# The experts' down product of a 256-slot block as seven products of halves instead of eight

## The chip, the core and the metric

The kernel runs on one core of a Trainium2 chip. The metric is the device time of one execution in microseconds. A core has five engines with queues of their own, each working in program order: TensorE (PE in the profile, its weight loads PEld), VectorE (DVE), ScalarE (ACT), GpSimd (POOL) and SyncE (SP). POOL and SP mostly issue DMAs here, which run on 16 shared DMA engines.

## The reference, cut to what matters

A two-layer network on 4 images of 32 x 32 tokens with 384 channels. The change lies in the feed-forward part of layer 0, a mixture of four experts of which each token takes two:

```python
def _L0_ffn_ref(x, gate_w, gate_b, w1, b1, w2, b2):
    ...
    topk_vals, topk_idx = jax.lax.top_k(probs, TOP_K)
    ...
    h = jax.nn.gelu(jnp.einsum('bsd,edh->ebsh', x, w1) + b1[:, None, None, :], approximate=False)
    y = jnp.einsum('ebsh,ehd->ebsd', h, w2) + b2[:, None, None, :]
    out = jnp.einsum('bse,ebsd->bsd', masked, y)
    return out
```

The hidden width is 1536. All numbers are float32. "Up" below is the product with `w1`, "down" the product with `w2`.

## The kernel before

The kernel runs attention of layer 0, then the experts, then layer 1 (`outlook`, and a last feed-forward part). The experts compute only the two chosen experts of each token. Every (token, expert) pair has a slot; slots of one expert lie together, in blocks of `XB` = 256, and there are `NXB` = 35 blocks. All 35 are run, one after another, by the loop over `n` in `experts` (from L1587 on).

What a block takes:

- `weights(n)` (L1524): two gathers by POOL bring the expert's `up` weights (128 x 4620 float32) and its `down` weights with the bias (128 x 4992 float32, 2.56 MB). There are two sets of these buffers, used in turn (`halves[n % 2]`), so weights of block n+2 can be fetched when their buffer is no longer read by block n.
- `tokens`, `fetch` (L1535, L1545): POOL gathers the slots' token numbers and the 256 rows of `x1` into `xb`.
- `norm` (L1554) on DVE scales them; `turn` (L1564, L1565) turns them on PE by six 128 x 128 transposes and copies them with DVE into `xbT`.
- Up: for each of the `NF` = 12 slices of 128 hidden units three products of 256 columns (L1607) into `ps_h`, then ACT's Gelu (L1611) into `h`. A float32 product is two matmul instructions, so this is 72 instructions.
- Down: for each half `t` of the block (128 slots) twelve products of 384 columns into one `ps_y` (L1624), 24 instructions a half. The stationary side is a 128 x 128 piece of `h`, the moving side a slice of `down`. DVE adds the bias (L1629), SP sends the half to `yg` in DRAM (L1630). `norm(n + 1)` stands ahead of the down part in DVE's queue, `turn(n + 1)` between the two halves in PE's.

Beside this run other pieces of work. In blocks 0 to 2, `beside` steps finish the attention's output and the routing (DVE L756 to L760 and others; the products L284 on PE). From block 16 on, once all blocks that a tile of 128 tokens needs are written, each block ends up with one `add(i)` (L1571 to L1578): SP loads a tile `x` of `x1` (L1572), POOL gathers the two experts' rows `yt` from `yg` (L1490), DVE forms the weighted sum (L1576, twice) and its statistics (L133, L134), and SP stores it (L1578) at the start of the next block. There are 19 such tiles in blocks 16 to 34; the rest is added in layer 1.

PE, DVE, ACT and SP keep the order in which the program is written (`manual_schedule`); POOL's order is chosen when the program is built. An instruction waits for its operands on its own engine's queue, and everything behind it on that engine waits too. So the order inside the loop matters: `add` is written before the up part, and its DVE instructions stand ahead of everything that DVE does later in the block.

Of the kernel before, what the change touches and what calls it, by code (L numbers as in the profile page):

```python
# [10 lines left out]
FP = mybir.dt.float32  # L11
BF = mybir.dt.bfloat16
AF = mybir.ActivationFunctionType
ALU = mybir.AluOpType
# [3 lines left out]
P = 128  # L18
B, IMG, C = 4, 32, 384
# [3 lines left out]
KC = C // P  # L23
# [3 lines left out]
NE, HID = 4, 1536  # L27
NF = HID // P
# [15 lines left out]
XB = 256  # L44
NXB = (2 * NT * P + NE * (XB - 1)) // XB
NFIRST = 4


class Net:
# [55 lines left out]
    def store(self, x):  # L105
        for b in range(B):
            self.nc.sync.dma_start(
                out=x[b * NTOK : (b + 1) * NTOK, :].rearrange("(t p) c -> p t c", p=P), in_=self.xs[b]
            )
# [1386 lines left out]
def experts(net, router, x1, x2, wup, wdown, beside):  # L1496

    tc, nc = net.tc, net.nc
    TT = XB // P
    I32 = mybir.dt.int32
    with ExitStack() as ctx:
        def pool(name, bufs, **kw):
            return ctx.enter_context(tc.tile_pool(name=name, bufs=bufs, reuse_waits="tile", **kw))


        halves = [pool(f"ex_{n}", 1) for n in range(2)]
        hp, work = pool("ex_h", 14), pool("ex_work", 4)
        ps_h, ps_y = pool("ex_ps_h", 3, space=PSUM), pool("ex_ps_y", 3, space=PSUM)

        def rows(n):
            w, t = router.firsts if n < NFIRST else router.all
            return w[:, n : n + 1], t[:, n : n + 1]

        def weights(n):  # L1520
            up = halves[n % 2].tile([P, KC * HID + NF], FP, name="up", tag="up")
            down = halves[n % 2].tile([P, NF * C + C], FP, name="down", tag="down")
            for t, w in ((up, wup), (down, wdown)):
                nc.gpsimd.indirect_dma_start(  # L1524
                    out=t, out_offset=None, in_=w,
                    in_offset=bass.IndirectOffsetOnAxis(ap=rows(n)[0], axis=0),
                )
            return up, down

        beside = beside(work)  # L1530
        ids, xbs = {}, {}

        def tokens(n):
            t = ids[n] = halves[0].tile([P, TT, router.LINE], I32, name="ids", tag="ids", bufs=6)
            nc.gpsimd.indirect_dma_start(  # L1535
                out=t.rearrange("p t w -> p (t w)"), out_offset=None,
                in_=net.table.rearrange("(r t) w -> r (t w)", t=TT),
                in_offset=bass.IndirectOffsetOnAxis(ap=rows(n)[1], axis=0),
            )

        def fetch(n):
            xb = xbs[n] = halves[n % 2].tile([P, TT, C], FP, name="xb", tag="xb")
            last = (B - 1 if n < NFIRST else B) * NTOK
            for t in range(TT):
                nc.gpsimd.indirect_dma_start(  # L1545
                    out=xb[:, t, :], out_offset=None, in_=x1[:last, :],
                    in_offset=bass.IndirectOffsetOnAxis(ap=ids[n][:, t, 0:1], axis=0),
                )

        def norm(n):  # L1550
            xb = xbs[n]
            own = ids.pop(n).bitcast(FP)
            for t in range(TT):
                nc.vector.tensor_scalar(  # L1554
                    xb[:, t, :], xb[:, t, :], own[:, t, 1:2], own[:, t, 2:3], ALU.subtract, ALU.mult
                )

        def turn(n):
            xb = xbs.pop(n)
            xbT = halves[n % 2].tile([P, KC, XB], FP, name="xbT", tag="xbT")  # L1560
            for t in range(TT):
                ps = router.psum()
                for c in range(KC):
                    nc.tensor.transpose(ps[:, c * P : (c + 1) * P], xb[:, t, c * P : (c + 1) * P], net.ident)  # L1564
                nc.vector.tensor_copy(  # L1565
                    xbT[:, :, t * P : (t + 1) * P], ps[:, :C].rearrange("p (c t) -> p c t", c=KC)
                )
            return xbT

        def add(i):  # L1570
            x = work.tile([P, C], FP, name="x", tag="x", bufs=2)  # L1571
            nc.sync.dma_start(out=x, in_=x1[i * P : (i + 1) * P, :])  # L1572
            for n in range(2):
                y = work.tile([P, C], FP, name="yt", tag="yt")
                router.gather(y, i, n)
                nc.vector.scalar_tensor_tensor(x, y, router.weight[n][:, i : i + 1], x, ALU.mult, ALU.add)  # L1576
            net.measure(work, i, x)
            return lambda: nc.sync.dma_start(out=x2[i * P : (i + 1) * P, :], in_=x)  # L1578

        added, store = 0, lambda: None  # L1580
        ws = {0: weights(0)}
        for n in range(NFIRST):
            tokens(n)
        fetch(0)
        norm(0)
        xbT = turn(0)
        for n in range(NXB):  # L1587
            if n == NFIRST - 1:
                for _ in beside:
                    pass  # L1590
            if n + 1 < NXB:
                if n + 1 >= NFIRST:
                    tokens(n + 1)
                ws[n + 1] = weights(n + 1)
                fetch(n + 1)
            store()
            store = lambda: None
            if n > router.complete(added // NB):
                store = add(added)
                added += 1  # L1600
            up, down = ws.pop(n)
            hs = []
            for f in range(NF):
                ps = ps_h.tile([P, XB], FP, name="ps_h", tag="h")
                for k in range(KC):
                    o = k * HID + f * P
                    nc.tensor.matmul(  # L1607
                        ps, lhsT=up[:, o : o + P], rhs=xbT[:, k, :], start=k == 0, stop=k == KC - 1,
                    )
                h = hp.tile([P, XB], FP, name="h", tag="h")  # L1610
                nc.scalar.activation(h, ps, AF.Gelu, bias=up[:, KC * HID + f : KC * HID + f + 1])  # L1611
                hs.append(h)
                if n < NFIRST - 1 and (n or f >= NF // 2):
                    next(beside, None)
            if n + 1 < NXB:
                norm(n + 1)
            else:
                net.scale(0, added)
            for t in range(TT):
                if t == TT - 1 and n + 1 < NXB:  # L1620
                    xbT = turn(n + 1)
                ps = ps_y.tile([P, C], FP, name="ps_y", tag="y")
                for f in range(NF):
                    nc.tensor.matmul(  # L1624
                        ps, lhsT=hs[f][:, t * P : (t + 1) * P], rhs=down[:, f * C : (f + 1) * C],
                        start=f == 0, stop=f == NF - 1,
                    )
                y = work.tile([P, C], FP, name="y", tag="y")
                nc.vector.tensor_tensor(y, ps, down[:, NF * C :], ALU.add)  # L1629
                nc.sync.dma_start(  # L1630
                    out=net.yg[n * XB : (n + 1) * XB, :].rearrange("(p t) c -> p t c", t=TT)[:, t, :], in_=y
                )
        store()
        return added

# [463 lines left out]
def metaformer_kernel(  # L2099
# [139 lines left out]
```

## Time and profile before

| what | number |
|---|---|
| median of 3 runs | 2905.45 us (2903.23 to 2907.56) |
| profiled execution, device time | 2905.3 us |
| its span, first to last instruction | 2903.6 us, 37519 instructions |
| mean granted PE clock | 0.965 |
| busy: PE, PEld | 2715.6 us (94%), 1453.0 us (50%) |
| busy: DVE, ACT, POOL | 1347.6 us (46%), 1208.3 us (42%), 401.3 us (14%) |
| DMA moved | 405.97 MB, mean 140 GB/s |
| experts, first up product to end of last down product | 1210.6 to 2345.6 us |

The page's busy time of an engine is the union of its instructions' times. The mean duration of a matmul in it contains the time in which it passes through the array while the next has begun, so the step from one matmul to the next is read from busy time over count, or from the starts in the timeline. A row of the groups reads: line, engine, operation, output <- inputs, shapes, count, busy time, mean duration, idle time of the engine just before, and what ended most of it. Idle time of an engine costs nothing unless another waits for it.

### The profile page before, as it was taken

What the parts mean: (1) busy time and instruction counts of PE and PEld (TensorE: products, weight loads), DVE (VectorE), ACT (ScalarE), POOL (GpSimd) and SP (SyncE); (2) the same over time, 40 slices, a digit from 0 to 9 for tenths busy, and PEclk for the clock granted to TensorE, in tenths of its full rate; (3) what the DMA queues carried; (4) which work ended last, traced back from release to release, by engine and by line L of the source; (5) the groups of instructions that cost most, each with busy time, mean ns of one, the idle gap of its engine ahead of it and who ended that gap; (6) DMA issues with size and microseconds to landing.
All of it is one profiled execution on the core that took longest, in us unless ns stands there. A gap on an engine that the chain in (4) does not pass through costs nothing. (4 is left out here: it accounts for less than half of the span.)

```text
span 2903.6 us, 37519 instructions
## 1 busy us (share of the span) xinstructions
PE 2715.6 (94%) x13632; PEld 1453.0 (50%) x13632; DVE 1347.6 (46%) x3714; ACT 1208.3 (42%) x2023; POOL 401.3 (14%) x500
## 2 busy tenths in 40 slices
PE   6889998999999987799999999999999999999988
PEld 3323333333333322367777777777777754444432
DVE  1377776777778786532010001111111146877642
ACT  3778777787778774212112111211211122122135
POOL 1000000120021004122111122212121101100000
PEclk9989999999999998799999999999999999999998
DMA  5143435222413334445545455555555437644432
GB/s 104 32 103 100 100 92 140 66 59 70 109 44 75 80 90 128 130 149 201 190 169 195 168 200 204 200 212 201 214 202 204 162 132 222 193 161 155 145 106 89
DMA packets 216996, 405.97 MB, mean 140 GB/s; under 512 B 83505, under 2 KB 177905, under 8 KB 203745
## 3 DMA queue, kind: packets, MB, share of 16 engines
q1 hardware_dynamic: 185504, 189.20, 22.2%
q0 software_dynamic: 27152, 209.66, 21.1%
q10 hardware_dynamic: 4144, 4.61, 0.5%
q8 instruction: 110, 1.80, 0.3%
q14 instruction: 86, 0.70, 0.1%
HBM read 305.35 MB, written 49.99 MB: 122 GB/s over the span
## 5 line engine op out<-in xcount | busy, mean ns | idle before, releaser
L1611 ACT ACTIVATE h<-ps_h,up 128x256 f32<-128x256 f32 x420 | 199.0, 474 | 916.5 <-PE ps_h L1607 916.4
L1607 PE MATMUL ps_h<-xbT,up 128*128 128x256 f32 x2520 | 553.5, 380 | 2.6 <-ACT h L1611 1.8
L1624 PE MATMUL ps_y<-down,h 128*128 128x384 f32 x1680 | 554.5, 487 | 0.0
L1607 PEld LDWEIGHTS ps_h<-xbT,up 128*128 128x128 f32 x2520 | 479.9, 191 | 77.9 <-ACT h L1611 2.7
L685 DVE CUSTOM_DVE_ANT_0 e<-e,rz,inv 128x1024 f32<-128x1024 f32 x384 | 475.2, 1274 | 51.8 <-DMA rz<-r_row 49.2
L633 ACT ACTIVATE e<-ps_s,ten 128x1024 f32<-128x1024 f32 x384 | 408.1, 1109 | 59.8 <-PE ps_s L623 36.2
L1624 PEld LDWEIGHTS ps_y<-down,h 128*128 128x128 f32 x1680 | 317.3, 191 | 207.0 <-issue 1.2
L1629 DVE TENSOR_TENSOR y<-ps_y,down 128x384 f32<-128x384 f32 x70 | 39.0, 557 | 718.1 <-PE ps_y L1624 718.1
L623 PE MATMUL ps_s<-q,k 32*128 32x512 f32 x1536 | 295.5, 667 | 53.4 <-ACT e L633 31.5
L641 PE MATMUL ps_o<-e,wv 128*32 128x512 f32 x1536 | 226.1, 664 | 40.5 <-DVE wv L692 39.0
L641 PE MATMUL ps_z<-e,rt_ones 128*32 128x512 f32 x1536 | 218.6, 643 | 0.0
L712 POOL DMA_DIRECT2D q<-po x96 | 76.1, 878 | 946.4 <-DMA q<-po 514.6
L369 ACT ACTIVATE below<-tk_left,tk_bound 128x1024 bf16<-128x1024 f32 (+1 forms) x160 | 184.3, 1152 | 52.3 <-DVE tk_bound L375 42.1
L623 PEld LDWEIGHTS ps_s<-q,k 32*128 32x128 f32 x1536 | 92.0, 189 | 192.2 <-ACT e L633 92.0
L1735 PE MATMUL ps_a<-wa,xnT 128*128 128x486 f32 x384 | 167.6, 585 | 8.7 <-DVE attn L1745 7.0
L284 PE MATMUL ps_t<-xnT,wqkv 128*128 128x512 f32 x288 | 137.1, 617 | 2.4 <-ACT xnT L466 1.7
L641 PEld LDWEIGHTS ps_o<-e,wv 128*32 128x32 f32 x1536 | 31.5, 111 | 199.7 <-issue 68.4
L1735 PEld LDWEIGHTS ps_a<-wa,xnT 128*128 128x128 f32 x384 | 71.7, 192 | 93.4 <-issue 85.3
L641 PEld LDWEIGHTS ps_z<-e,rt_ones 128*32 128x32 f32 x1536 | 52.3, 117 | 132.0 <-issue 128.7
L1576 DVE SCALAR_TENSOR_TENSOR x<-yt,weight,x 128x384 f32<-128x384 f32 x38 | 23.5, 619 | 188.3 <-DMA x<-x 187.6
L1837 PE MATMUL ps_y<-band,v 128*32 128x194 f32 (+2 forms) x960 | 102.7, 517 | 8.0 <-DMA band<-room 7.7
L1490 POOL DMA_INDIRECT yt<-yg,index x64 | 65.5, 1024 | 305.9 <-DVE x L1576 142.4
(346 smaller groups left out, 2739.5 us busy)
## 6 DMA issues: line engine op xcount, KB each, us to landing
band<-room SPq DMA_DIRECT2D x32, 1560.0 KB
rz<-r_row SPq DMA_DIRECT2D x48, 512.0 KB
yg<-y SPq DMA_DIRECT2D x70, 192.0 KB
q<-q SPq DMA_DIRECT2D x192, 64.0 KB
k<-k SPq DMA_DIRECT2D x192, 64.0 KB
room<-none SPq DMA_DIRECT2D x64, 192.0 KB
x<-x SPq DMA_DIRECT2D x38, 192.0 KB
o<-in_x_dram SPq DMA_DIRECT2D x33, 192.0 KB
```

Source lines behind the costliest of these rows:

```text
L284: nc.tensor.matmul(ps, lhsT=lhsT(k), rhs=rhs(k), start=k == 0, stop=k == KC - 1)
L369: nc.scalar.activation(junk[:n], left[:n], AF.Sign, bias=bound[:n], accum_out=over[:n])
L623: nc.tensor.matmul(ps[:, half * 512 : half * 512 + 512], lhsT=self.k4[r, u * P : (u + 1) * P], rhs=self.q4[r, :], start=True, stop=True,)
L633: nc.scalar.activation(e, ps, AF.Exp, bias=shift, scale=QK_SCALE)
L641: nc.tensor.matmul(ps[r : r + 32, :], lhsT=lhsT(odd), rhs=self.es[2 * u + odd][:, half * 512 : half * 512 + 512], start=u == 0, stop=u == ...
L685: nc.vector.tensor_tensor_reduce(self.es[m], self.es[m], self.rz, 1.0, self.im["inv"][:, m, self.h : self.h + 1], ALU.mult, ALU.add, self. ...
L712: nc.gpsimd.dma_start(out=there, in_=po[r : r + 32, :], accum_op=ALU.add)
L1607: nc.tensor.matmul(ps, lhsT=up[:, o : o + P], rhs=xbT[:, k, :], start=k == 0, stop=k == KC - 1,)
L1611: nc.scalar.activation(h, ps, AF.Gelu, bias=up[:, KC * HID + f : KC * HID + f + 1])
L1624: nc.tensor.matmul(ps, lhsT=hs[f][:, t * P : (t + 1) * P], rhs=down[:, f * C : (f + 1) * C], start=f == 0, stop=f == NF - 1,)
L1735: nc.tensor.matmul(pa[:, hh, :HW_], lhsT=xnT[:, k, :], rhs=wa[:, k, hh * HW_ : (hh + 1) * HW_], start=k == 0, stop=k == KC - 1,)
L1837: nc.tensor.matmul(ys[c][32 * n : 32 * n + 32, lo - 512 * half : hi - 512 * half], lhsT=vs[b, t][:, h * HD : (h + 1) * HD], rhs=bands[b, t ...
```

## The change

With the block's `h` cut into halves of slots (t) and of hidden units (c), and `down` into halves of hidden units (k) and of output columns (c), the down part is a product of two 2 x 2 matrices of blocks: eight products of 128 slots x 768 hidden units x 192 columns. Before, they are done as 24 float32 products of 384 columns. After, seven products of 192 columns (12 matmul instructions each) are done, on sums of quarters:

- `folded(down)`: four sums of weight quarters (`t1` to `t4`, 128 x 1152 each) and the difference of the two bias halves (`shift`), on DVE, at the start of the block's up part, behind `add`.
- `paired(one, two, g)`: four sums of quarters of `h` (128 x 384 each), twice a block, on DVE: for hidden slices 0-2 with 6-8, and for 3-5 with 9-11. The up part takes the slices in the order 0-2, 6-8, 3-5, 9-11, so that the first pair is there after six of twelve slices.
- `total`: nine sums of 128 x 192 on DVE put the products together, seven of them reading a product's PSUM tile (three such tiles, as before).
- `h` is kept as tiles of three slices, five of them; `y` in two tiles by name.
- The first half of `y` is sent after the fifth product, which is followed by `turn(n + 1)`; the second after the seventh.
- The `down` buffer is read by the first, second and fifth product, by `folded` and by the first `total`; products three, four, six and seven read the sums.

```diff
-        hp, work = pool("ex_h", 14), pool("ex_work", 4)
+        hp, work, sums = pool("ex_h", NG3 + 1), pool("ex_work", 4), pool("ex_sums", 1)
...
+        def folded(down):
+            w11, w12, w21, w22 = (quadrant(down, k, c) for k in range(2) for c in range(2))
+            t = sums.tile([P, 4, HF, D], FP, name="wsum", tag="wsum")
+            t1, t2, t3, t4 = (t[:, i] for i in range(4))
+            nc.vector.tensor_tensor(t1, w12, w11, ALU.subtract)
+            nc.vector.tensor_tensor(t2, w22, t1, ALU.subtract)
+            nc.vector.tensor_tensor(t3, w22, w12, ALU.subtract)
+            nc.vector.tensor_tensor(t4, w21, t2, ALU.subtract)
...
+        def paired(one, two, g):
+            s = sums.tile([P, 4, 3, P], FP, name=f"hsum_{g}", tag=f"hsum_{g}")
+            a11, a21, a12, a22 = (h[:, :, t * P : (t + 1) * P] for h in (one, two) for t in range(TT))
+            s1, s2, s3, s4 = (s[:, i] for i in range(4))
+            nc.vector.tensor_tensor(s1, a21, a22, ALU.add)
+            nc.vector.tensor_tensor(s2, s1, a11, ALU.subtract)
+            nc.vector.tensor_tensor(s4, a12, s2, ALU.subtract)
+            nc.vector.tensor_tensor(s3, a11, a21, ALU.subtract)
+            return s
...
             up, down = ws.pop(n)
-            hs = []
-            for f in range(NF):
+            w11, w21, w22, t1, t2, t3, t4, shift = folded(down)
+            hs, ss = [None] * NG3, []
+            for f in (*range(0, 3), *range(6, 9), *range(3, 6), *range(9, 12)):
...
+                if f in (8, 11):
+                    g = len(ss)
+                    ss.append(paired(hs[g], hs[g + 2], g))
...
-            for t in range(TT):
-                if t == TT - 1 and n + 1 < NXB:
-                    xbT = turn(n + 1)
-                ps = ps_y.tile([P, C], FP, name="ps_y", tag="y")
-                for f in range(NF):
-                    nc.tensor.matmul(
-                        ps, lhsT=hs[f][:, t * P : (t + 1) * P], rhs=down[:, f * C : (f + 1) * C],
-                        start=f == 0, stop=f == NF - 1,
-                    )
-                y = work.tile([P, C], FP, name="y", tag="y")
-                nc.vector.tensor_tensor(y, ps, down[:, NF * C :], ALU.add)
...
+            def product(left, right):
+                ps = ps_y.tile([P, D], FP, name="ps_y", tag="y")
+                for f in range(HF):
+                    nc.tensor.matmul(ps, lhsT=left[f], rhs=right[:, f, :], start=f == 0, stop=f == HF - 1)
+                return ps
...
+            total(c21, product(a(0, 0), w11), down[:, NF * C : NF * C + D])
+            total(c11, product(a(1, 0), w21), c21)
+            total(c22, product(s(0), t1), shift)
+            total(c21, product(s(1), t2), c21)
+            total(c12, c21, c22)
+            total(c12, product(s(3), w22), c12)
+            send(0)
+            if n + 1 < NXB:
+                xbT = turn(n + 1)
+            total(c21, product(s(2), t3), c21)
+            total(c22, c21, c22)
+            total(c21, product(a(1, 1), t4), c21)
+            send(1)
```

More of the change, by code (lines that the diff above doesn't have):

```diff
@@ L1506, in experts @@
     I32 = mybir.dt.int32
+    D, HF = C // 2, NF // 2
+    NG3 = NF // 3
     with ExitStack() as ctx:
@@ L1578, in add, with quadrant @@
             return lambda: nc.sync.dma_start(out=x2[i * P : (i + 1) * P, :], in_=x)
+        def quadrant(down, k, c):
+            w = down[:, : NF * C].rearrange("p (k f c d) -> p k f c d", k=2, f=HF, c=2)
+            return w[:, k, :, c, :]
+        def folded(down):
[6 more added lines that the diff above has]
+            nc.vector.tensor_tensor(t4, w21, t2, ALU.subtract)
+            shift = sums.tile([P, D], FP, name="shift", tag="shift")
+            low, high = (down[:, NF * C + c * D : NF * C + (c + 1) * D] for c in range(2))
+            nc.vector.tensor_tensor(shift, high, low, ALU.subtract)
+            return w11, w21, w22, t1, t2, t3, t4, shift
+        def paired(one, two, g):
[7 more added lines that the diff above has]
+            return s
         added, store = 0, lambda: None
@@ L1609, in experts @@
                     )
[L1610 to L1613, printed above, removed]
+                if f % 3 == 0:
+                    hs[f // 3] = hp.tile([P, 3, XB], FP, name="h", tag="h")
+                nc.scalar.activation(
+                    hs[f // 3][:, f % 3, :], ps, AF.Gelu, bias=up[:, KC * HID + f : KC * HID + f + 1]
+                )
+                if n < NFIRST - 1 and (n or f % 6 >= 3):
                     next(beside, None)
+                if f in (8, 11):
+                    g = len(ss)
+                    ss.append(paired(hs[g], hs[g + 2], g))
             if n + 1 < NXB:
@@ L1618, in experts, with a, s, total @@
                 net.scale(0, added)
-            for t in range(TT):
-                if t == TT - 1 and n + 1 < NXB:
-                    xbT = turn(n + 1)
-                ps = ps_y.tile([P, C], FP, name="ps_y", tag="y")
-                for f in range(NF):
-                    nc.tensor.matmul(
-                        ps, lhsT=hs[f][:, t * P : (t + 1) * P], rhs=down[:, f * C : (f + 1) * C],
-                        start=f == 0, stop=f == NF - 1,
-                    )
-                y = work.tile([P, C], FP, name="y", tag="y")
-                nc.vector.tensor_tensor(y, ps, down[:, NF * C :], ALU.add)
+            ys = [work.tile([P, C], FP, name=f"y{t}", tag=f"y{t}", bufs=2) for t in range(TT)]
+            (c11, c12), (c21, c22) = ((y[:, :D], y[:, D:]) for y in ys)
+            def a(c, t):
+                return [hs[f // 3 + 2 * c][:, f % 3, t * P : (t + 1) * P] for f in range(HF)]
+            def s(i):
+                return [ss[f // 3][:, i, f % 3, :] for f in range(HF)]
+            def product(left, right):
[3 more added lines that the diff above has]
+                return ps
+            def total(out, one, two):
+                nc.vector.tensor_tensor(out, one, two, ALU.add)
+            def send(t):
                 nc.sync.dma_start(
-                    out=net.yg[n * XB : (n + 1) * XB, :].rearrange("(p t) c -> p t c", t=TT)[:, t, :], in_=y
+                    out=net.yg[n * XB : (n + 1) * XB, :].rearrange("(p t) c -> p t c", t=TT)[:, t, :], in_=ys[t]
                 )
+            total(c21, product(a(0, 0), w11), down[:, NF * C : NF * C + D])
[11 more added lines that the diff above has]
+            send(1)
         store()
```

## The prediction

> **What bounds the kernel now.** First the page's slices and groups. The experts take 1210.6 to 2345.6 us, slices 17 to 32 of 40; there PE stands at 9, and its clock at 9.
>
> ```profile
> PE   6889998999999987799999999999999999999988
> PEclk9989999999999998799999999999999999999998
> ...
> L1607 PE MATMUL ps_h<-xbT,up 128*128 128x256 f32 x2520 | 553.5, 380 | 2.6 <-ACT h L1611 1.8
> L1624 PE MATMUL ps_y<-down,h 128*128 128x384 f32 x1680 | 554.5, 487 | 0.0
> ...
> L1624 PEld LDWEIGHTS ps_y<-down,h 128*128 128x128 f32 x1680 | 317.3, 191 | 207.0 <-issue 1.2
> L1629 DVE TENSOR_TENSOR y<-ps_y,down 128x384 f32<-128x384 f32 x70 | 39.0, 557 | 718.1 <-PE ps_y L1624 718.1
> ...
> L1576 DVE SCALAR_TENSOR_TENSOR x<-yt,weight,x 128x384 f32<-128x384 f32 x38 | 23.5, 619 | 188.3 <-DMA x<-x 187.6
> ```
>
> PE waited 0.0 us ahead of the down matmuls, while DVE waited 718.1 us for them: PE sets the pace. Next, one block cut at its parts, in the view of stretches (start:end, length, then busy time and count of PE, PEld, DVE, ACT, POOL, granted clock, DMA share, GB/s):
>
> ```profile
> 1807.52:1823.06 15.54, 15.54 (x74) 13.68 (x73) 3.29 (x7) 5.21 (x11) 3.44 (x4) 1.00 0.59 216
> 1823.06:1830.80 7.74, 7.74 (x26) 4.51 (x25) 0.00 (x0) 0.48 (x1) 1.54 (x2) 1.00 0.79 281
> 1830.80:1831.45 0.65, 0.65 (x7) 0.65 (x6) 0.45 (x1) 0.00 (x0) 0.00 (x0) 1.00 0.99 426
> 1831.45:1839.19 7.74, 7.74 (x26) 4.57 (x25) 1.03 (x3) 0.00 (x0) 1.89 (x2) 1.00 0.29 93
> ```
>
> Up takes 15.54 us (72 instructions, 216 ns each), each half of down 7.74 (24, 322.5 ns), the transposes 0.65: 31.67 us a block, PE busy in all of it at full clock. DVE has 26.9 us of it free. So the chain of waits, which holds only the end of the run, is not needed: a block is as long as PE's stream, until another engine makes PE wait.
>
> **What PE loses.** Down falls from 48 instructions of 384 columns (15.48 us) to 7 x 12 = 84 of 192. The whole change hangs on the step of one of these. Bounds: 162 ns if the columns bind (384 columns take 322.5, 256 take 216: 0.84 ns a column), 191 ns if a weight load binds, since each needs its own 128 x 128 load and that row has 191 ns. The nearest rows are short runs with as many columns and full loads, in the timeline of PE (start, length, line, count):
>
> ```profile
> 2696.79 0.47 PE L1800 MATMUL ps_c<-u,shift 128*128 128x180 f32 x2
> 2697.09 0.47 PE L1800 MATMUL ps_c<-u,shift_-1_15514 128*128 128x180 f32 x2
> 2697.40 0.47 PE L1800 MATMUL ps_c<-u,shift 128*128 128x180 f32 x2
> 2697.70 0.49 PE L151 MATMUL ps_tr<-ident,xn 128*128 128x128 f32 x3
> ```
>
> From 2696.79 to 2697.70 six go by: 152 ns each at 180 columns, though their six loads are 187 to 190 ns long. Loads thus overlap one another, and 191 is a length, not a step. At 192 columns (L569) a run of four spans 0.81 us; less the last one's 326 ns, three steps are 161 ns each. I take **162.5 ns**.
>
> A rule speaks against this: the Trainium skill, "TensorE: Matmul & The Clock Gate", section "Back-to-back issue gap", says that a sustained stream of load and matmul pairs at 128 columns steps by about 81 ns, where columns alone give 56. Those 25 ns on each instruction make 187.5 ns, 84 x 0.1875 = 15.75 us, 0.27 more than before: nothing gained, +9 us over 35 blocks. The row has no such surcharge (152 for 180 columns), but is only six long. I go with the row: 84 x 0.1625 = 13.65 us, **1.83 us less a block**, 29.84 us instead of 31.67. Groups of twelve and their waits cost nothing if these are met: up's twelve groups each wait for a PSUM tile and still step at 216.
>
> **What DVE gains, and whether PE feels it.** Durations: a sum of two SBUF operands takes 0.88 us at 700 columns (L1419) and 0.49 at 324 (L1752), so columns/0.96 + 0.155. Four sums of 1152 take 1.355 each, a little less apart when independent: with `shift` 5.6 us. `paired`: 0.555 each, 2.2 a call, twice. A `total` about 0.36 (150 columns from PSUM take 0.306, L1808), nine are 3.2. The old two adds (1.1) go. DVE rises from 4.8 to about 17 us a block, far below 29.8; only its order can hurt. Count from the block's start T (first up matmul).
>
> Without `add` and `beside` (blocks 3 to 15): the last `total` ends at T+0.56, `folded` at 6.2; the sixth Gelu ends at 8.5 (first starts at T+1.54, then every 1.295), first `paired` at 10.8; the twelfth Gelu ends at 16.3, second `paired` at 18.5, its first sum at 16.9; `norm` (0.84) at 19.4, first `total` at 19.75. PE starts product three, which needs that first sum, at 15.54 + 2 x 1.95 = 19.44, and product four, which needs the first `total` to have freed its PSUM tile, at 21.39. Nothing stalls, by 1.6 us.
>
> With `add` (blocks 16 to 34) DVE first stands at L1576 until `x` is in. Call that T+X. Weighted sums and statistics take 2.0 (1819.07 to 1821.07), then `folded`, both `paired`, `norm`, `total`: the first `total` ends at X + 2.0 + 5.6 + 4.4 + 0.85 + 0.4 = X + 13.25. PE waits at product four if **X is over 8.1**, and a block then loses X - 8.1. Before, X is 11.55, and it cost nothing, since only `norm` stood behind it, needed at T+23:
>
> ```profile
> 1808.54 0.94 POOL L1524 DMA_INDIRECT down<-in_wdown_dram,rows_w_all  x1 [6.14 <-DVE y L1629]
> 1808.67 0.42 SPq L1578 DMA_DIRECT2D x<-x  x1
> ...
> 1809.19 0.39 SPq L1572 DMA_DIRECT2D x<-x  x1
> ...
> 1819.07 1.27 DVE L1576 SCALAR_TENSOR_TENSOR x<-yt,weight,x 128x384 f32<-128x384 f32 x2 [10.79 <-DMA x<-x]
> ```
>
> The load of `x` is issued at T+1.7, behind SP's send and store, just after the 2.56 MB of `down` (issue to landing 10.0 us), and lands with its end. In block 16, where nothing is stored and the load goes out in the same instant as `down`, it lands in 2.6 us. The change moves `down`: its buffer is free after product five, T+25.4, no longer after the block's last add. POOL's order in the built program is up, ids, down, xb, xb, yt, yt (before: xb, xb, down, yt, yt, ids, up), so `down` is issued at 25.6, and lands at 35.6, which is T'+5.8 of the next block (T' = T + 29.84). The gathers of `xb` and `yt` are issued behind it, until T'+0.6; their rows take some 2.4 and 1.5 us of all DMA engines (DMA shares at 1831 to 1836 and 1820 to 1824). Ends for X: 4.2 (no backlog, as in block 16) and 10 (the load behind all of that and three transfers of SP of 0.5 each). `yt` is gathered a block ahead and doesn't matter. I take 6 to 8, nearest to the row in which `x` lands with the end of `down`: **no stall**. `down` itself is needed earlier than before, at T by `folded` instead of at T+15.5, but lands 24 us ahead of that.
>
> **The first blocks lose**, because there DVE has other work and the sums queue with it. Block 0: DVE waits for loads of `o` until 1249.8 (L756), and PE stood 3.93 us for `norm`. Now the second `paired` comes between the two: product three starts at about 1251.7 after 8 us of idle, and PE restarts slow (behind the old idle, half of down took 9.23 instead of 7.9, the transposes 1.26 instead of 0.82): the block ends some 2.3 us later than at 1261.8. Block 1: `folded` delays the routing's DVE work, for which ACT and PE already stood 1.77 us, by about 1 us: gain 0.8. Block 2: DVE works on routing from 1301.35 to 1318.29, 17 us from its start on (L1437 to L1481), and both `paired` stand behind all of that in its order. `folded` to T+6.2, routing to 23.2, first `paired` 25.4, first sum of the second 26.0: product three starts at 26.0 instead of 19.44, again slow (1.7 us), and the block takes about 26.0 + 3.6 + 4 x 1.95 + 0.65 = 38.05 instead of 31.67: 6.4 lost. Blocks after the experts are unchanged: their loads waited for block 33's buffers, which come free no later.
>
> Sum: 32 x 1.83 + 0.8 - 2.3 - 6.4 = 50.7 us. From the profiled execution's own 2905.3 (1.7 above its span, 0.15 below the median shown): **2855 us**.
>
> **Rivals.** (1) **Slower at its end**: X lands late, and blocks 17 to 33 (in block 34 no `down` follows) lose X - 8.1 each, PE standing for DVE's sums at product four. At X = 10 that is 32 us, 2887; at the old 11.5 it is 58 us, 2913. It decides from X = 8.1 + 50.7/17 = 11.1 on. For it: `x` landed at the very end of what was queued, and so far always ten microseconds after its issue but in blocks 16 and 34. Against: most of `down` is now through when it is issued. Chance 0.20, of which 0.03 over 2911. (2) **Slower**: weight loads bind in long runs at the row's 191 ns: 84 x 0.191 = 16.04, 2.39 a block above the forecast, 84 us: 2938. It decides from a step of 180 ns on (0.1625 + 50.7/2940). For it: the rule above; against: six loads at 152. Chance 0.10. (3) The sums run longer than priced, DVE's strided reads or POOL's descriptor work in their way: at X = 7 the chain to product four has 1.1 us in hand out of 13, so from 10% on it costs, perhaps 1 us in each of 17 blocks and more in block 2: 2875. Chance 0.08. The forecast keeps 0.62.
>
> Range: the forecast's own goes from 2845 (the first blocks lose nothing but gain little) to 2866; with rival three, and rival one at X = 10, up to 2888. What a measurement here tells from no change is 0.2%, 6 us. Chances: faster 0.83 (forecast, rival three, most of rival one), within 0.04 (rival one near 11), slower 0.13 (its end, and rival two).
>
> **What would show it.** The down group's busy time over its 2940 instructions at 0.163 us (right) or 0.19 (rival two); block starts 29.8 us apart; no idle time of PE ahead of products three and four in blocks 17 to 33, with L1576 starting before T+8.1 (rival one: idle of PE released there by DVE's sums or totals); `down` issued by POOL on release by PE's fifth product; stops of PE ahead of product three in blocks 0 and 2, of 8 and 6.6 us.

## The result, and the profile after

| | before | after |
|---|---|---|
| median | 2905.39 us (2903.23 to 2907.56, 4 runs) | 2860.62 us (2856.08 to 2863.53, 4 runs) |
| ratio, 95% interval | | 0.9844 (0.9827 to 0.9862) |
| profiled execution, its span | 2905.3, 2903.6 us | 2862.9, 2861.2 us |
| experts, first up product to end of last down product | 1210.6 to 2345.5 us | 1217.4 to 2303.6 us |
| from the end of block 0 to that end | 1083.8 us | 1040.8 us |

The device time fell by 1.6%. The last row of the table is the one to compare. The experts' first up product started anywhere from 1207.8 to 1217.4 us in the traces of this study (those with narrowed down products left aside), while block 0 ended between 1260.3 and 1265.9: most of the shift is taken up again in block 0, which waits on VectorE for the attention's last loads `o` (until 1249.8 us before and 1249.7 after). The end of block 0 moves by several microseconds from run to run, and no run here says why; the stretch behind it is steadier.

First the slices and groups of the page of the kernel after (busy time, mean ns of one | idle time just before, and what ended it):

```profile
PE   6889998999999997699999999999999989999988
...
DVE  1377677677767787666544545554554567777642
...
PEclk9989999999999997699999999999999999999999
...
L1637 PE MATMUL ps_h<-xbT,up 128*128 128x256 f32 x2520 | 554.1, 380 | 2.5 <-ACT h L1642 1.8
L1666 PE MATMUL ps_y<-wsum,hsum 128*128 128x192 f32 x1260 | 224.0, 331 | 12.4 <-DVE y L1670 7.2
...
L1666 PEld LDWEIGHTS ps_y<-wsum,hsum 128*128 128x128 f32 x1260 | 207.5, 192 | 17.7 <-DVE y L1670 10.7
...
L1666 PE MATMUL ps_y<-down,h 128*128 128x192 f32 x840 | 142.2, 326 | 0.0
```

PE still stands at 9 in the experts and the up group is unchanged. The down products that read the sums (`wsum`, `hsum`) now have idle time ahead of them, 12.4 us, put down mostly to VectorE's `total`s; those that read `down` and `h` have none. The group also has a longer mean (331 ns against 326): some of the lost time hides inside its instructions.

Then an undisturbed block (18) cut at its parts, in the view of stretches (start:end, length, then busy time and count of PE, PEld, DVE, ACT, POOL, clock, DMA share, GB/s):

```profile
1786.80:1802.34 15.54, 15.54 (x74) 13.69 (x73) 7.71 (x11) 5.21 (x11) 2.95 (x2) 1.00 0.56 205
1802.34:1812.09 9.75, 9.75 (x62) 9.73 (x61) 6.62 (x16) 0.47 (x1) 1.91 (x2) 1.00 0.64 244
1812.09:1812.74 0.65, 0.65 (x7) 0.65 (x6) 0.45 (x2) 0.00 (x0) 0.22 (x1) 1.00 0.00 0
1812.74:1816.64 3.90, 3.90 (x26) 3.90 (x25) 1.61 (x4) 0.00 (x0) 2.62 (x3) 1.00 0.77 235
```

Five products take 9.75 us and two take 3.90: 3.90 / 24 = 162.5 ns an instruction. The block is 29.84 us, 1.83 less than before. PEld is busy in all of the last stretch and PE loses nothing by it.

A block in which `add` stands in the way, block 17, which begins at 1754.96. PE's timeline (start, length, line, count, idle time before it):

```profile
1754.96 15.70 PE L1637 MATMUL ps_h<-xbT,up 128*128 128x256 f32 x72
1770.50 4.06 PE L1666 MATMUL ps_y<-down,h 128*128 128x192 f32 x24
1774.40 2.38 PE L1666 MATMUL ps_y<-wsum,hsum 128*128 128x192 f32 x12
1778.24 2.22 PE L1666 MATMUL ps_y<-wsum,hsum 128*128 128x192 f32 x12 [1.46 <-DVE y L1670]
1780.29 2.11 PE L1666 MATMUL ps_y<-down,hsum 128*128 128x192 f32 x12
```

and VectorE's in the same block:

```profile
1765.36 1.27 DVE L1578 SCALAR_TENSOR_TENSOR x<-yt,weight,x 128x384 f32<-128x384 f32 x2 [9.85 <-DMA x<-x]
...
1767.37 1.33 DVE L1590 TENSOR_TENSOR wsum<-down 128x1152 f32<-128x1152 f32 x1
...
1772.81 0.55 DVE L1603 TENSOR_TENSOR hsum<-h 128x384 f32<-128x384 f32 x1
...
1777.05 0.86 DVE L1556 TENSOR_SCALAR xb<-xb,ids 128x384 f32<-128x384 f32 x2
1777.84 0.34 DVE L1670 TENSOR_TENSOR y<-ps_y,down 128x192 f32<-128x192 f32 x1
```

VectorE stood for 9.85 us until `x` had landed, at X = 10.40 (X is the time from the block's start to L1578). Then everything runs without a gap: the first `total` ends at 1778.18, X + 12.82, and 0.06 us later PE starts product four. A block is longer by about X - 8.4: 2.0 us here, 0 where X is 8.1. Over blocks 17 to 33 X lies between 7.5 and 10.4, and these blocks together are 7.6 us over 29.85 each (7.7 with block 16).

What was issued ahead of that `x`, in the timelines of POOL and of SP:

```profile
1750.84 0.94 POOL L1526 DMA_INDIRECT down<-in_wdown_dram,rows_w_all  x1 [3.56 <-PE ps_y L1666]
1752.08 0.95 POOL L1547 DMA_INDIRECT xb<-x,ids  x1 [0.30 <-issue]
1753.34 0.95 POOL L1547 DMA_INDIRECT xb<-x,ids  x1 [0.30 <-issue]
```

```profile
1756.40 0.49 SPq L1574 DMA_DIRECT2D x<-x  x1
```

`down` goes out when product five of block 16 has released its buffer, 5.6 us ahead of `x`, and the rows of `xb` go out behind it.

The blocks, from start to start:

| block | before | after |
|---|---|---|
| 0 | 51.21 | 45.40 (began 6.8 us later, ended 1.0 later) |
| 1 | 38.91 | 37.01 |
| 2 | 31.67 | 37.19 |
| 3 to 15 | 31.68 | 29.85 |
| 16 to 33 | 31.68 | 29.84 to 31.84 |
| 34 | 31.17 | 33.67 |

So of 32 x 1.83 = 58.6 us, blocks 16 to 33 gave back 7.7, block 34 4.3 (it was counted with a gain of 1.83 and lost 2.50), block 2 lost 5.5, and block 1 gained 1.9: 43.0, as the table of the result has it.

Block 34 is the surprise. What POOL and SP issued at its start, 2269.91, in the timeline of each (POOL first):

```profile
2265.57 0.36 POOL L1777 MEMSET down<- 32x324 f32 x1 [6.88 <-PE ps_y L1666]
...
2266.18 0.98 POOL L99 DMA_DIRECT2D x<-x  x1
2267.15 0.81 POOL L2197 DMA_DIRECT2D wa<-in_WaT_dram  x1
```

```profile
2265.93 4.87 SPq L1673 DMA_DIRECT2D yg<-y  x2
2270.86 0.47 SPq L1580 DMA_DIRECT2D x<-x  x1
2271.42 0.39 SPq L1574 DMA_DIRECT2D x<-x  x1
```

Once PE had done product five of block 33, POOL was free to issue the loads for layer 1, 1.5 MB of `x` (L99) and `wa`. The `x` of the block's `add` (L1574) is issued 5.2 us behind them, and was used at X = 11.7. Before, both went out in the same instant:

```profile
2315.77 0.98 POOL L99 DMA_DIRECT2D x<-x  x1
```

```profile
2316.03 0.39 SPq L1572 DMA_DIRECT2D x<-x  x1
```

and X was 4.3.

### The profile page after: what moved, and what is told of

Same layout as the page of the kernel before. It is cut to its first block, busy times and chain, and to the rows that moved or that the text cites. A ratio compares the mean times of both kernels' runs of the same rounds, so it can differ in the third digit from the quotient of the medians.

```text
span 2861.2 us, 40451 instructions
## 1 busy us (share of the span) xinstructions
PE 2664.1 (93%) x14892; PEld 1617.2 (57%) x14892; DVE 1754.3 (61%) x4414; ACT 1206.8 (42%) x2023; POOL 419.8 (15%) x500
## 5 line engine op out<-in xcount | busy, mean ns | idle before, releaser
L633 ACT ACTIVATE e<-ps_s,ten 128x1024 f32<-128x1024 f32 x384 | 407.8, 1108 | 69.8 <-PE ps_o L641 36.1
L1666 PE MATMUL ps_y<-wsum,hsum 128*128 128x192 f32 x1260 | 224.0, 331 | 12.4 <-DVE y L1670 7.2
L1666 PEld LDWEIGHTS ps_y<-wsum,hsum 128*128 128x128 f32 x1260 | 207.5, 192 | 17.7 <-DVE y L1670 10.7
L369 ACT ACTIVATE below<-tk_left,tk_bound 128x1024 bf16<-128x1024 f32 (+1 forms) x160 | 184.3, 1152 | 52.7 <-DVE tk_bound L375 41.7
L1670 DVE TENSOR_TENSOR y<-ps_y,y 128x192 f32<-128x192 f32 x175 | 62.5, 357 | 188.2 <-PE ps_y L1666 184.5
L1666 PE MATMUL ps_y<-down,h 128*128 128x192 f32 x840 | 142.2, 326 | 0.0
L1666 PEld LDWEIGHTS ps_y<-down,h 128*128 128x128 f32 x840 | 138.4, 190 | 2.0
L1490 POOL DMA_INDIRECT yt<-yg,index x64 | 78.4, 1226 | 328.8 <-DVE x L1578 135.1
```

The costliest lines, as they stand in the source:

```text
L369: nc.scalar.activation(junk[:n], left[:n], AF.Sign, bias=bound[:n], accum_out=over[:n])
L633: nc.scalar.activation(e, ps, AF.Exp, bias=shift, scale=QK_SCALE)
L1490: self.nc.gpsimd.indirect_dma_start(out=y, out_offset=None, in_=self.net.yg[: self.complete(i // NB) * XB, :], in_offset=bass.IndirectOffs ...
L1666: nc.tensor.matmul(ps, lhsT=left[f], rhs=right[:, f, :], start=f == 0, stop=f == HF - 1)
```

## Experiments

The theory after this: PE's stream of 29.85 us a block is as predicted, and all that was given back comes from VectorE's program order. Sums stand behind `x` in the add blocks and behind routing in block 2. Rivals: the sums are simply too much work; VectorE's traffic disturbs PE; weight loads set part of the step.

**fold_first**: `folded` ahead of `add`.

```diff
-            if n > router.complete(added // NB):
-                store = add(added)
-                added += 1
             up, down = ws.pop(n)
             w11, w21, w22, t1, t2, t3, t4, shift = folded(down)
+            if n > router.complete(added // NB):
+                store = add(added)
+                added += 1
```

> The sums of weights go ahead of the add on VectorE, so they no longer stand behind x. Theory (x lands late, and everything on VectorE stands behind the add): first total at X + 7.7 us after the block's start instead of X + 12.8, so X may be 13.5; blocks 17 to 33 all at 29.85 us (7.8 us gained over the changed kernel), block 34 about 29.85 instead of 33.5 (3.6 gained); expert stage about 1074.6 us instead of 1086.0. Rival (VectorE's sums are simply too long, or DMA traffic disturbs TensorE's reads): the long blocks of 30.2 to 31.8 us stay, stage 1086.

Measured: 2855.41 us, ratio to before 0.9821 (0.9800 to 0.9843); from the end of block 0 1028.8 us, 12.0 less than after; blocks 16 to 33 29.85 each, block 34 29.35. The whole stage (1080.9) missed the expected 1074.6, since block 0 took 52.2 us here and 45.4 in the trace after; the stretch behind it moved by what was expected (11.4) and half a microsecond more. `x` was as late as ever (X from 7.7 to 9.7). Block 34, which begins at 2265.35, in VectorE's timeline:

```profile
2269.75 1.35 DVE L1593 TENSOR_TENSOR wsum<-down,wsum 128x1152 f32<-128x1152 f32 x1
...
2276.93 1.27 DVE L1578 SCALAR_TENSOR_TENSOR x<-yt,weight,x 128x384 f32<-128x384 f32 x2 [5.55 <-DMA x<-x]
...
2281.59 0.56 DVE L1603 TENSOR_TENSOR hsum<-h 128x384 f32<-128x384 f32 x1 [0.48 <-ACT h L1642]
...
2283.91 0.29 DVE L1670 TENSOR_TENSOR y<-ps_y,down 128x192 f32<-128x192 f32 x1
```

The wait for `x` is still there at X = 11.58, but the weights' sums are done ahead of it. The second `paired` now waits for ScalarE's last Gelu, where Gelu's results had waited for VectorE, and the first `total` ends at X + 7.27, in time.

**early_x**: the order of VectorE as in the kernel after, but SP loads each `x` one block ahead, with a third buffer.

```diff
+        def early(i):
+            x = ready[i] = work.tile([P, C], FP, name="x", tag="x", bufs=3)
+            nc.sync.dma_start(out=x, in_=x1[i * P : (i + 1) * P, :])
+
         def add(i):
-            x = work.tile([P, C], FP, name="x", tag="x", bufs=2)
-            nc.sync.dma_start(out=x, in_=x1[i * P : (i + 1) * P, :])
+            x = ready.pop(i)
...
+                if added == 0:
+                    early(0)
+                if n + 1 < NXB:
+                    early(added + 1)
                 store = add(added)
```

> Only the load of x moves: issued one block ahead, with a third buffer; VectorE's order is that of the changed kernel. Theory (the landing of x decides): L1578 starts within 3 us of the block's start, no idle of TensorE at products three and four, blocks 17 to 34 at 29.85 us, stage about 1074.6 us. Rival (VectorE's chain as such, 12.8 us behind x, is what is late; or the gathered rows yt are late too): L1578 starts later than 5 us after the block's start and part of the 11 us stays.

Measured: 2850.40 us, 0.9814 (0.9789 to 0.9839); from the end of block 0 1028.95 us. L1578 starts 0.5 us after the block's start in blocks 17 to 34, which all take 29.85 (34: 29.35). Only block 16, whose `x` is still loaded in the block itself, has X = 8.7 and 30.16 us. So the landing of `x` is the late thing, and `yt` is not late. Either remedy recovers the same 12 us. The two traces are 7.5 us apart; 5.7 of these lie in block 0's end (1265.9 and 1260.3), 1.9 in what follows the experts, and none in these blocks. Block 0 (52.4 us) is also why the stage took 1081.4 and not 1074.6.

**late_loads**: the three loads for layer 1 go from POOL to SP, behind block 34's `x`.

```diff
-            net.load(x2, range(NB), tc.nc.gpsimd)
-            weigh(tc.nc.gpsimd, wa, WaT)
-            weigh(tc.nc.gpsimd, wv, WvT)
+            net.load(x2, range(NB))
+            weigh(tc.nc.sync, wa, WaT)
+            weigh(tc.nc.sync, wv, WvT)
```

> The changed kernel, with the three loads for what follows the experts (x of 1.5 MB, wa, wv) issued by SyncE behind the load of x of block 34 instead of by GpSimd ahead of it; the order of TensorE's instructions stays. Theory (those loads make block 34's x late): L1578 in block 34 starts within 6 us of the block's start instead of 11.7, block 34 takes about 29.4 us instead of 33.7; what comes after may begin some 5 us later, since wa is then loaded last. Rival (x is late there for another reason, such as its own queue): X stays over 10, block 34 over 32 us.

Measured: block 34 has X = 4.1 and takes 29.35 us. With the 1.5 MB issued 0.5 us behind `x` instead of 5.2 us ahead of it, and `wa` and `wv` after that, `x` is there in time: the loads of layer 1 made it late. As a version it is no good: layer 1 then waits 6.7 us for `wa`, and the run took 2875.27 us (a single run; blocks 1 and 2 were 1.2 and 1.9 us longer there too, for which I have no reason).

**old_block2**: block 2 alone by the old eight products (24 of 384 columns), without sums.

```diff
+            if not (n == 2):
-            w11, w21, w22, t1, t2, t3, t4, shift = folded(down)
+                w11, w21, w22, t1, t2, t3, t4, shift = folded(down)
...
-                if f in (8, 11):
+                if f in (8, 11) and not (n == 2):
...
+            if n == 2:
+                for t in range(TT):
...
+                    nc.vector.tensor_tensor(ys[t], ps, down[:, NF * C :], ALU.add)
+                    send(t)
```

> Block 2 alone is computed by the old eight products, without sums. Theory (its sums stand behind 17 us of routing work on VectorE): block 2 takes about 31.7 us instead of 37.2, stage 1080.5 us instead of 1086.0, all other blocks as they were. Rival (the routing work itself holds TensorE up, through the normalization or the transposes): block 2 stays over 34 us.

Measured: block 2 takes 31.68 us instead of 37.19. The time, 2859.04 us, 0.9835 (0.9809 to 0.9860), shows little of these 5.5 us, because blocks 16 to 33 gave back 12.2 us in this trace instead of 7.7: `x` landed later (X up to 10.8). From the end of block 0 it took 1039.5 us, only 1.3 less than after, and the stage (1092.1) missed the expected 1080.5, block 0 alone being 7.3 us longer. So "all other blocks as they were" did not hold, and the edit is read from its own block. What block 2 looked like in the kernel after, in PE's timeline:

```profile
1315.34 4.06 PE L1666 MATMUL ps_y<-down,h 128*128 128x192 f32 x24
1323.55 4.41 PE L1666 MATMUL ps_y<-wsum,hsum 128*128 128x192 f32 x12 [4.15 <-DVE hsum L1603]
1328.43 2.22 PE L1666 MATMUL ps_y<-wsum,hsum 128*128 128x192 f32 x12 [0.47 <-DVE y L1670]
```

Product three waits 4.15 us for the first sums of `h`, then takes 4.41 us instead of 2.11, since it meets the second `paired` half way.

**no_sums**: the sums of quarters are left out, and the seven products are made of raw quarters; products and totals stay.

```diff
-            t = sums.tile([P, 4, HF, D], FP, name="wsum", tag="wsum")
...
+            t1, t2, t3, t4, shift = w12, w22, w12, w21, down[:, NF * C : NF * C + D]
...
-                    ss.append(paired(hs[g], hs[g + 2], g))
...
-                return [ss[f // 3][:, i, f % 3, :] for f in range(HF)]
+                return a(*((0, 1), (1, 1), (0, 0), (1, 0))[i])
```

> The seven products are made of raw quarters: the sums of quarters of h and of weights are left out (so the output is that of another formula), all products and totals stay. Theory (TensorE's stream is 29.85 us a block, all else is waiting for sums): blocks 2 to 34 all at 29.85 us, stage 1086.0 - 7.8 - 3.6 - 7.3 = about 1067 us, some 19 us less than the changed kernel. Rival (weight loads or clock set part of the 29.85, or the totals delay TensorE): blocks 17 to 34 stay above 30 in part, stage above 1075.

Measured: 2842.24 us, 0.9783 (0.9759 to 0.9806); from the end of block 0 1021.5 us, 19.3 less than after; blocks 2 to 33 29.85 each. (The stage, 1073.1, again holds a longer block 0.) X was 10.9 to 13.9 in blocks 16 to 33 and cost nothing, since no sums stood behind it. It is as late as before the change: product seven reads `down` itself here, so POOL issues the next `down` 0.4 us after the block's start, and not 4.1 us ahead of it as in the kernel after. This agrees with the prediction that the earlier release of `down` brings `x` forward. The shorter stream alone is thus worth 1083.8 - 1021.5 = 62.3 us in this stretch, and the sums took 19.3 of it back. Block 1 takes 37.02 here too: there the sums cost nothing.

**sums_only**: the old eight products in every block, with all sums computed and not used.

```diff
-            total(c21, product(a(0, 0), w11), down[:, NF * C : NF * C + D])
...
+                for t in range(TT):
+                    if t == TT - 1 and n + 1 < NXB:
+                        xbT = turn(n + 1)
...
+                    nc.vector.tensor_tensor(ys[t], ps, down[:, NF * C :], ALU.add)
+                    send(t)
```

> The old eight products in every block, with all sums of quarters computed on VectorE and not used. Theory (the sums cost only where VectorE's order makes TensorE wait): blocks 3 to 15 stay at 31.67 us; block 2 about 5 us longer, and the add blocks about 1 us longer each, because the normalization behind the sums comes at X + 12.9, that is at 24.4 for X = 11.55, and is needed at 23.3; from the end of block 0 about 1108 us against 1083.8 before. Rival (VectorE's traffic in SBUF slows TensorE's reads or the weight loads): blocks 3 to 15 longer than 31.7 us.

Measured: 2926.61 us (a single run); from the end of block 0 1103.6 us, 19.8 more than before (1108 were expected). The same stretch of time in this kernel and in the kernel before, among blocks 3 to 15:

```profile
1450.00:1481.67 31.67, 31.67 (x127) 23.41 (x126) 12.55 (x19) 5.68 (x13) 5.80 (x5) 1.00 0.48 181
```

```profile
1450.00:1481.67 31.67, 31.67 (x127) 23.41 (x126) 2.82 (x6) 5.69 (x12) 4.73 (x5) 1.00 0.49 182
```

VectorE works 12.55 us instead of 2.82, and PE does exactly the same number of instructions: no disturbance shows. Blocks 3 to 15 stay at 31.68. Block 2 takes 39.24 (7.6 longer; 5 was expected, PE idle 4.5 and then slow), blocks 17 to 33 0.4 to 2.2 longer, 12.4 us together. The sums cost through their place in the order, not through their work.

**thin96, thin128, thin64**: the kernel before, with each half of the down product in groups of W columns, so that each weight load serves fewer columns.

```diff
-                ps = ps_y.tile([P, C], FP, name="ps_y", tag="y")
-                for f in range(NF):
...
+                W = 96
+                for q in range(0, C, W):
+                    ps = ps_y.tile([P, W], FP, name="ps_y", tag="y")
+                    for f in range(NF):
...
```

> The kernel before, with each half of the down product in four column groups of 96: 192 recorded instructions a block of 96 columns, each with its own 128 x 128 weight load. Theory (columns set the step, loads overlap one another): 82.5 ns each, 15.84 us a block, blocks of 32.0 us. Rival of a surcharge of 25 ns on each pair: 107.5 ns, 20.6 us, blocks of 36.8 us. Rival of loads that cannot overlap (191 ns each): 36.7 us, blocks of 52.9 us. In between, a floor of the step by the load would show as a step over 85 ns; then 192 columns lie above that floor, since they step at 162.5.

Measured: 3107.86 us (a single run), blocks of 37.61 us. In the timeline of PE, one half of down:

```profile
1813.24 10.85 PE L1627 MATMUL ps_y<-down,h 128*128 128x96 f32 x96
1823.93 0.82 PE L1564 MATMUL ps_t<-ident,xb 128*128 128x128 f32 x6
```

From 1813.24 to 1823.93 are 10.69 us for 96 instructions, 111.4 ns each: neither the columns (82.5) nor the length of a load (its mean is 193 in the groups), and near the surcharge (107.5). One size can't tell a surcharge from a floor, so two more were run.

> As thin96, with three groups of 128 columns: 144 recorded instructions a block. thin96 stepped at 111.4 ns where columns alone make 82.5, with PEld busy all the time. Theory (a floor of about 111 ns by the weight load, below which columns don't count): 111.4 ns or little more, 16.04 us a block, blocks of 32.2 us. Rival (a surcharge of 25 to 29 ns on each pair that fades only above 128 columns): 107.5 + 25 to 29 = 132 to 136 ns, blocks of 35.3 to 35.9 us.

> As thin96, with six groups of 64 columns: 288 recorded instructions a block. Theory (floor by the load): 111.4 ns again, 32.1 us a block, blocks of 48.3 us. Rival (surcharge on top of columns): 53.8 + 29 = 83 ns, 23.8 us, blocks of 40.0 us.

Measured: 2921.20 and 3479.69 us (a single run each), blocks of 32.27 and 48.31 us. A half of down, for 128 columns

```profile
1740.59 8.20 PE L1627 MATMUL ps_y<-down,h 128*128 128x128 f32 x72
1748.63 15.71 PE L1607 MATMUL ps_h<-xbT,up 128*128 128x256 f32 x72
```

and for 64:

```profile
1743.71 16.19 PE L1627 MATMUL ps_y<-down,h 128*128 128x64 f32 x144
1759.74 5.62 PE L1607 MATMUL ps_h<-xbT,up 128*128 128x256 f32 x25
```

8.04 / 72 = 111.7 ns and 16.03 / 144 = 111.3 ns. The step doesn't depend on the columns from 64 to 128: it is a floor, not a surcharge. With 0.84 ns a column it would be met at about 133 columns (an estimate; no width between 128 and 180 was run), and 192 lie above it. That the load is what sets the floor is not shown, since no run changed the load alone. A pair of load and matmul as such can go faster: in the attention of the kernel before, pairs with 128 x 128 bfloat16 loads and 4 columns (L419) start 25 to 27 ns apart.

**combo**: fold_first and old_block2 together.

> Both remedies together: sums of weights ahead of the add, and block 2 by the old eight products. If the losses add (theory): from the end of block 0 to the last product 1028.8 - 5.5 = 1023.3 us, against 1040.8 in the changed kernel and 1083.8 before; time about 2860.6 - 17.5 = 2843 us, give or take the 5 us by which block 0's end moves between runs. Rival (part of what fold_first gained comes back elsewhere): over 1027 us for the stretch.

Measured: 2846.04 us, 0.9773 (0.9751 to 0.9795); from the end of block 0 1023.3 us, as the sum had it. The waits of PE in that stretch, in the view of waits of the kernel after (total, times, longest):

```profile
PE ps_y L1666 <- DVE y L1670: 6.2, 9, 1.5
PE ps_y L1666 <- DVE hsum L1603: 5.2, 3, 4.1
PE ps_h L1637 <- ACT h L1642: 1.8, 1, 1.8
```

and of combo:

```profile
PE ps_h L1638 <- ACT h L1643: 1.8, 1, 1.8
PE ps_t L1326 <- DVE rt_run L1320: 0.2, 1, 0.2
```

Both waits for sums are gone. The stretch is 1.8 us longer than without any sums, which is the 1.83 that block 2 doesn't gain. It is faster than both kernels, and the expected 2843 us was 3 short.

**after_again**: the kernel after once more, beside combo.

> The changed kernel once more, for how much of the difference is chance: the end of block 0 between 1260 and 1266 us, whenever the experts start; from there 1041 us (1039 to 1043); block 2 37.2, block 34 33.6, long blocks among 17 to 33 in other places, since they come from the landing of x.

Measured: 2864.16 us, 0.9846 (0.9829 to 0.9864), so combo is 18.1 us faster on the same chip (17.5 were expected). From the end of block 0 1042.95 us; block 2 37.22, block 34 33.66; blocks 16 to 33 gave back 9.8 us instead of 7.7. "In other places" missed: the eight blocks that were over 30 us in the first trace (17, 20, 24, 25, 27, 28, 31, 32) are over 30 here too, and X of blocks 17 to 33 goes with that of the first trace (correlation 0.91). So how late `x` is depends mostly on the block, and less on chance.

## Why the prediction was right, and where it was off

The forecast was 2855 us, the profiled execution took 2862.9, and the median is 2860.62. The main mechanism was right: PE's stream sets the pace, and the narrower products step by their columns. Of the add blocks the forecast was wrong that they don't stall. The sum of 50.7 us came out as 42.4, by these steps:

- **The step of 162.5 ns** was right to the digit, as was the block of 29.84. The six instructions of 180 columns in layer 1 told the truth about 2940 of them, and the length of a load (191) is not its step. The rule of the Trainium skill that was weighed against the row, "TensorE: Matmul & The Clock Gate", "Back-to-back issue gap", is given for 128 columns; carried over to 192 it made an estimate of 187.5 ns, which is not what this step shows. Yet thin96 shows that there is something behind it: below about 133 columns the pair of load and matmul sets 111.5 ns. The same page's section "LDWEIGHTS (loading the stationary operand)" gives a load as columns / 1.2 ns, an estimate of 107 for 128, close to the measured floor. So for these float32 products the form that fits is the larger of the two, not their sum. Rival two is refuted at this size.
- **No stall in the add blocks** failed: "I take 6 to 8, nearest to the row in which `x` lands with the end of `down`". X was 7.5 to 10.4. What was behind `x` was priced well (X + 13.25 predicted to the end of the first `total`, X + 12.8 measured; so the bound is 8.4, not 8.1). `down` was issued at T+25.7 of the block before (25.6 predicted), and SP issued `x` 1.4 us after the block's start. It then took 9 us to land in block 17. The mis-sized term is this landing: by 2 us, worth 7.7 us in all. This is rival one at its mild end (it was priced at 32 us for X = 10 in all seventeen blocks; 10 was reached in one).
- **Where these 2 us lie** is told by the records of DMA packets in the trace of the kernel after. `down` came where it was put: in block 33, where no `xb` follows it, its last packet was through at T+5.6 (5.8 predicted). But `x` doesn't land with it. SP's queue moved no packet from T to T+4.0 in any of blocks 17 to 33, though the second half of `y` was issued at T+0.6 and `x` at T+1.4. And behind `down` the rows of `xb` were still coming: the last packet of GpSimd's queue ahead of L1578 was through at T+6.6 in block 18 (X = 8.05), at 7.8 in block 24 (9.18), at 9.2 in block 17 (10.40). Over blocks 17 to 33 X is 1.2 to 2.6 us behind that packet, and it is lowest in block 33, which has no `xb` behind `down`. The forecast tied `x` to the end of `down`; the rows behind it stood only in its upper end, X = 10. (The rows `yt`, which it also put there, are issued at T+7.9 or later.) No run moved `xb`, so this is read from packets and not shown by an experiment.
- **"Blocks after the experts are unchanged: their loads waited for block 33's buffers, which come free no later"** failed as to block 34: they come free *earlier*, and there the loads get ahead of `x`. Block 34 was counted with a gain of 1.83 and lost 2.5: 4.3 us. The same release that helped the weights in the other blocks, product five, did this; late_loads, early_x and fold_first each take the loss away.
- **Block 2** was predicted at 38.05 and took 37.19. The routing ended where it was put (T+23.2 predicted, 1322.94 is T+23.1). Product three began earlier, since its first half needs only the first `paired`, and was then slower for lack of the second.
- **Block 1** gained 1.9 instead of 0.8; no_sums shows the same 37.0, so no delay by `folded` reaches its end.
- **Block 0** can't be judged: 2.3 us of loss were predicted, its end came 1.0 later, and that end moves by more than this between runs. The stop of 8 us ahead of product three isn't in this trace, where the block began 6.8 us later and its up part ran until 1247.2; in the trace of fold_first PE stood for 5.7 us in the middle of product three.
- **Rival three**, sums longer than priced, is refuted: 1.33 to 1.36 and 0.55 us were measured for 1.355 and 0.555.

Together: -7.7 (adds), -4.3 (block 34), +0.9, +1.1 (blocks 2 and 1), +1.3 (end of block 0), +0.5 (after the experts) are -8.2 of the 8.3 by which the sum was off. The last two, 1.8 us, are within what moves from run to run: that much closeness is luck.

What stays open: why the rows of `xb` take longer in some blocks than in others, and why SP's queue moves nothing before T+4. Two runs of this kernel gave back 7.7 and 9.8 us in blocks 16 to 33, mostly in the same blocks. In old_block2, with the same code in these blocks, it was 12.2; block 18 has X = 10.8 there and 11.1 in combo, the two runs with a shorter block 2, against 8.1 to 8.6 in after, after_again, fold_first and late_loads. No run separated the transfers ahead of `x` within blocks 17 to 33.

## What to carry to other kernels

When work moves to an engine with room, its total is not the question: place it in that engine's program order and ask what stands in front, above all a wait for a DMA; here 12 us came back by moving five instructions ahead of such a wait, or by loading one block earlier. A buffer that comes free earlier lets its next load go earlier, and here that load came ahead of a small one that something waited for; follow each release to what it triggers. Before products are cut into more and narrower ones, find the step at that width by a run of instructions with full loads in the trace: here it was the larger of the columns' time and a floor.

## What the runs showed of the hardware

- A stream of float32 matmul instructions, each with its own 128 x 128 weight load, steps at 111.3 to 111.7 ns for 64, 96 and 128 columns, and at 162.5, 216 and 322.5 ns for 192, 256 and 384. A load's length in the trace has a mean of 190 to 193 ns in all of these, longer than the step up to 192 columns, so loads overlap one another there.
- PEld busy all the time is no sign that loads bind: it was busy for 3.90 of 3.90 us at 192 columns, where the columns set the step, and for 10.69 of 10.69 at 96, where the floor does. Steps tell it, busy shares don't.
- VectorE's 9.7 us more of reading and writing SBUF in 31.67 us changed nothing in PE's stream (127 instructions in both rows), and neither in the clock (1.00 in both).
- One tile of 128 x 384 loaded by SP was in use 2.6 us after its issue with none of GpSimd's bulk loads ahead of it (block 34 of late_loads), and 9.0 and 10.2 us after it where 2.9 and 3.7 MB of them had been issued within the 6 us before (blocks 17 and 34 of the kernel after: `down` with `xb`, and `x`, `wa` and `wv`).
